# One product of a projection and one transpose in another order, and other matmuls ahead of the first slot

## Chip, core and metric

The kernel runs on one core of a Trainium2 chip. The metric is the device time in microseconds (us), the median of several runs. In the profile PE is TensorE's matmuls, PEld its weight loads, DVE is VectorE, ACT is ScalarE, POOL is GpSimd and SP is SyncE, which here only issues transfers. L474 is line 474 of the kernel before the change.

## The reference

One transformer block on 8 sequences of 256 tokens with 512 features, all in float32:

```python
def _L0_attn_ref(hidden_states, w_qkv, w_o):
    ...
    qkv = hidden_states @ w_qkv
    q = qkv[..., :NH * D].reshape(B, S, NKV, G, D)
    k = qkv[..., NH * D:NH * D + NKV * D].reshape(B, S, NKV, D)
    v = qkv[..., NH * D + NKV * D:].reshape(B, S, NKV, D)
    scores = jnp.einsum('bqhgd,bkhd->bhgqk', q, k) * scale
    ...
    bias = -slopes[:, :, None, None] * sqrt_dist
    bias = jnp.where(rel[None, None] >= 0, bias, -jnp.inf)
    attn = jax.nn.softmax(scores + bias[None], axis=-1)
    out = jnp.einsum('bhgqk,bkhd->bqhgd', attn, v).reshape(B, S, NH * D)
    return out @ w_o
...
x = x + _L0_attn_ref(_layernorm(x, axis=-1), L0_attn_w_qkv, L0_attn_w_o)
x = x + _L0_ffn_ref(_layernorm(x, axis=-1), L0_ffn_weight, L0_ffn_bias, L0_ffn_centroids, L0_ffn_assignments)
```

There are 32 query heads in 8 groups of 4, each group with one head of keys and values, and D is 128. The second half is a dense 512 x 512 layer whose rows and columns are masked by a softmax over 64 centroids.

## The kernel before, in words

**Work and slots.** The tokens are handled in 4 pairs of sequences (`p`), and within a pair by group of heads (`kv`). A pair and a group make a `g` (32 of them), and `g` with one of its two sequences (`bb`) makes a unit `u` (64). The main loop runs over `u`; one turn is called a slot, and `slot = u % 16` is its place in its pair. Even slots have `bb == 0`. A slot works on three units at once: the scores of unit `u`, the softmax of unit `u - 1`, and the attention product and output projection of unit `u - 2`.

**Order.** The order of every engine's queue is written by hand (`manual_schedule`): an engine runs its instructions in the order in which the calls stand in the loop's body, and semaphores make it wait for the others. The body is a list of short calls: `e(i)` and `qq(i)` are steps of the projections to keys or values and to queries, `av(i)` (`attend`) the two attention products, `w(i)` steps of the output projection, `f` and `norm` steps of the feed-forward layer and the layer norm, `x(i)` transposes of the next pair's tokens.

**Products.** Each projection is done in Strassen's form (Winograd's variant), with seven block products instead of eight. Its factors are blocks and sums of blocks (`FACTORS`, L130). For the output projection (`project_out`, L461) these are:

- product 1: raw blocks of oT and wo, bank `ps_oa`; ACT copies it to `snap` (L489)
- product 2: raw blocks too, bank `ps_ob`; DVE adds it to x2 (L494)
- product 5: first sum of oT (POOL, L112) by a sum of wo, bank `ps_oc`; DVE adds it (L500)
- products 6, 7 and 4: accumulated into `ps_oa` after each copy of it; product 3: accumulated into `ps_oc`.

oT is written by DVE (L456) out of the attention products, times one over the sums of the softmax. `av(1)` then gives POOL the four sums of oT (L112 to L118). Banks of PSUM for `av`, product 2, product 5 and the like come from one pool of three that rotate; `aw`, `aq` and `tp` have one bank each.

**Joint transpose.** `max_and_old` and `sum_old` leave DVE's maxima of unit `u` and sums of unit `u - 1` in one tile r (L393, L394, L396). `rows()` (`over_quadrants`, L399) has PE transpose both at once (tp_r, L403), DVE reduce them (L407, L410), and SP write them to HBM (row_hbm, L412) and read them back broadcast over all partitions (bc, L421). In the next slot POOL (L428) and DVE (L431) subtract the maxima, ACT takes exp (L759), and L456 uses the sums.

**Tail of a slot.** Before the change, an even slot ends with

```python
            f(2), norm(0), e(5), e(4), qq(6), e(3), x(0), w(1), x(1), sum_old(), w(5, 6), norm(1), qq(7), w(2)
            rows(), behind_rows(), w(7, 3), norm(3), w(4)
```

and an odd one likewise, with `qq(3)` in place of `qq(7)`. `qq(7)` is drained by an ACT copy, `qq(3)` by a DVE add (L170).

**Start.** While the first tokens and weights load, PE multiplies a 128 x 128 tile of ones by itself 14 times (L625) into `tp1`. Then it transposes the first tokens (L296) once `xn` is there, and the first projection to keys needs wk from HBM.

Of the kernel before, what the change touches and what calls it, by code (L numbers as in the profile page):

```python
# [25 lines left out]
P = 128  # L26
# [27 lines left out]
def block_kernel(  # L54
# [12 lines left out]
    nc = tc.nc  # L67
# [177 lines left out]
    ones = const.tile([P, P], F32, name="ones")  # L245
# [10 lines left out]
    def norm_stats(*tiles):  # L256

        n = len(tiles)
        mv = small.tile([P, 2, 2], F32, tag="mv", name="mv", bufs=2)[:, :n]
        for j, t in enumerate(tiles):  # L260
            stats = small.tile([P, 6], F32, tag="stats", name=f"stats_{t}")
            nc.vector.bn_stats(stats, x2[t])
            nc.vector.bn_aggr(mv[:, j], stats)
        return mv, tiles

    def norm_root(found):

        mv, tiles = found
        rstd = small.tile([P, 2], F32, tag="rstd", name="rstd", bufs=2)[:, : len(tiles)]
        nc.scalar.activation(rstd, mv[:, :, 1], AF.Sqrt, bias=eps)  # L270
        return mv, tiles, rstd
# [49 lines left out]
    def project_v(p, half, i):  # L321

        if i == 0:
            v_sb[p, half] = work.tile([P, TPP, 512], F32, tag="v", name="v", bufs=2)
        v = v_sb[p, half]
        return strassen("v", "aw", wv[p, half], xB[p],
                        lambda w, x: [(slice(0, HH), x[:, c, ts(i, P)], w[:, c, :]) for c in range(2)],
                        [v[:, n * 2 + i, ts(m, HH)] for m in range(2) for n in range(2)], HH)

    def project_k(p, j):  # L330

        kT = kT_sb[p, j] = work.tile([P, 2, PT_TOK], F32, tag="kT", name="kT", bufs=2)
        return strassen("k", "aw", wk[p, j], xB[p],
                        lambda w, x: [(slice(0, S), w[:, c, :], x[:, c, :]) for c in range(2)],
                        [kT[:, m, ts(n, S)] for m in range(2) for n in range(2)], S)
# [175 lines left out]
    def ffn_transpose(t, tag="xnT", **kw):  # L511
        xnT_sb[t] = work.tile([P, NC_H, P], F32, tag=tag, name=f"xnT_{tag}")
        transpose_into(xnT_sb[t], xn_sb[t], t, **kw)
# [19 lines left out]
    def ffn_second(t, w_ffn):  # L533

        second = p_sc.tile([P, 512], F32, tag="sc", name="ps_lg")
        ffn_product(t, w_ffn, HH, HH + NCL, second)
        ffn_sb[t] = second[:, HH : HH + NCL]
        y_sb[t] = [None, second[:, :HH]]

    def ffn_first(t, w_ffn):  # L540
        first = p_acc.tile([P, 512], F32, tag="acc", name="ps_f")
        ffn_product(t, w_ffn, 0, HH, first)
        y_sb[t][0] = first[:, :HH]
# [77 lines left out]
    nc.scalar.activation(warm, eps, AF.Sqrt)  # L621
    tp1 = p_sc.tile([P, 512], F32, tag="sc", name="tpx_1")
    tp2 = p_sc.tile([P, 512], F32, tag="sc", name="tpx_2")
    for i in range(14):
        nc.tensor.matmul(tp1[:, :P], lhsT=ones, rhs=ones, start=True, stop=True)  # L625
    found0 = norm_root(norm_stats(0))
    found1 = norm_root(norm_stats(1))
    norm_write(norm_scale(found0))
# [33 lines left out]
    for u in range(NU + 2):  # L662
        g, bb = divmod(u, 2)
        p, kv = divmod(g, NKV)
        slot = u % SPP
# [19 lines left out]
        e, qq = nothing, nothing  # L685
        if own and u > 0 and slot in (0, 1, 8, 9):
            e = project_v(p, slot // 8, bb)
        elif own and slot in (3, 7, 11):
            e = project_k(p, (slot + 1) // 4)
        elif more_p and slot == 15:  # L690
            e = project_k(p + 1, 0)
        if more_q:
            if bb == 0:
                q = project_q(g + 1)
            qq = q
        ww = {}

        def w(*steps):
            for i in steps:
                if out_:  # L700
                    if i == 1:
                        ww[0] = project_out(u - 2)
                    ww[0](i)


        t_ffn = None
        if own and 3 <= slot < 7 and 0 < p < NPAIR - 1:
            t_ffn = (p - 1) * TPP + slot - 3
        if u >= NU - 2:
            t_ffn = first_late + u - (NU - 2)  # L710

        def f(part):
            if t_ffn is not None:
                if part == 0:
                    ffn_transpose(t_ffn)
                elif part == 1:
                    ffn_second(t_ffn, w_ffn)
                elif part == 1.5:
                    ffn_first(t_ffn, w_ffn)
                    ffn_max(t_ffn)  # L720
                    ffn_exp(t_ffn)
                elif part == 2:
                    ffn_bias_add(t_ffn, y_late[:, t_ffn % TPP, :] if t_ffn >= first_late else None)
                else:
                    ffn_hits(t_ffn)
                    ffn_qsel(t_ffn)
                    ffn_end(t_ffn)
# [12 lines left out]
        def norm(part):  # L740
            nonlocal found
            if t_norm is not None:
                found = (lambda _: norm_stats(t_norm, t_norm + 1), norm_root, norm_scale, norm_write)[part](found)
# [17 lines left out]
        def sum_old():  # L761
            if old:
                over_keys(s_sb[u - 1], r, 1, ALU.add)
# [3 lines left out]
        def rows_max():  # L767
            if alone:
                over_quadrants(u, r, True, False)

        def rows():
            if old:
                over_quadrants(u, r, own and not alone, True)

        def behind_rows():

            f(3)
            norm(2)
            if own and (slot == 7 or slot == 15 and more_p):
                sum_weights(ve, wv, (p, 1) if slot == 7 else (p + 1, 0), HH, "S1 S2")  # L780
            if more_p and slot == 13:
                sum_x(p + 1, "T1 T2")
# [7 lines left out]
        def x(i):  # L790
            if more_p and slot in (11, 12):
                norm_tile(p + 1, 2 * (slot - 11) + i)

        if u == 0:
            k(3), max_and_old()
            sum_weights(ve, wv, (0, 0), HH, "")
            e = project_v(0, 0, 0)
            q_first("5p"), e(1), q_first(5), e(2), rows_max(), q_first(3)
            a_sums(ve, wv[0, 0])
            qq(1), e(6), qq(2), e(7), e(5), qq(6), e(4), e(3), qq(7)  # L800
        elif u == 1:
            e(1), qq(4), e(2), max_and_old(), sum_old(), e(6), qq(5), e(7), e(5), e(4), e(3), qq(3), rows()
        elif bb == 0 and own:
            qq(1), e(1), max_and_old(), e(2), f(0), av(0), e(6), exp_old(), av(1), more_sums(), f(1), rows_max(), f(1.5), e(7), qq(2)
            if u == 4:
                onehot_of_columns(asg)
            f(2), norm(0), e(5), e(4), qq(6), e(3), x(0), w(1), x(1), sum_old(), w(5, 6), norm(1), qq(7), w(2)
            rows(), behind_rows(), w(7, 3), norm(3), w(4)
        elif u < NU - 1:
            e(1), qq(4), e(2), max_and_old(), f(0), e(6), av(0), exp_old(), e(7), av(1), f(1), f(1.5), e(5), qq(5)  # L810
            f(2), norm(0), e(4), e(3), x(0), w(1), x(1), sum_old(), w(5, 6), norm(1), qq(3), w(2)
            rows(), behind_rows()
            if u == NU - 3:
                found_late = norm_scale(norm_root(found_late))
            w(7, 3), norm(3), w(4)
        elif own:

            max_and_old(), f(0), av(0), exp_old(), av(1), rows_max(), f(1), f(1.5)
            f(2), w(1), sum_old(), w(5, 6), w(2)
            rows(), subtract_max(u, 0), subtract_max(u, 1)  # L820
            w(7)
            norm_write(found_late)
            nc.scalar.activation(s_sb[u], s_sb[u], AF.Exp)
            w(3), w(4)
            t_old = t_ffn
        elif bb == 0:
            sum_old(), av(0), f(0), av(1), f(1), rows()
            ffn_first(t_ffn, w_ffn), w(1, 5)
            ffn_max(t_ffn), ffn_exp(t_ffn)
            f(2), w(6)  # L830
            flush_adds()
            ffn_hits(t_old), ffn_qsel(t_old), ffn_end(t_old)
            w(2, 7)
            flush_adds()
            w(3, 4)
            found = norm_stats(last, last + 1)
            t_old = t_ffn
        else:
            av(0), f(0), ffn_hits(t_old), ffn_qsel(t_old)
            found = norm_scale(norm_root(found))  # L840
            av(1), norm_write(found, tags=("y", "y")), f(1), ffn_end(t_old)
            ffn_max(t_ffn), ffn_exp(t_ffn)
            w(1, 2, 5, 6, 3)
            found = norm_root(norm_stats(last + 2))
            w(7)
            ffn_transpose(last, "bc")
            ffn_transpose(last + 1, "snap", tp=p_long.tile([P, 512], F32, tag="aq", name="tpx_late"))
            norm_write(norm_scale(found))
            ffn_hits(t_ffn), w(4), ffn_qsel(t_ffn)
            normalise(norm_stats(last + 3))  # L850
            ffn_first(t_ffn, w_ffn)
# [145 lines left out]
```

## Time and profile before

| what | value |
|---|---|
| median of 3 runs (lowest to highest) | 1418.16 us (1415.27 to 1418.52) |
| the profiled execution, and its span | 1418.65 us, 1416.8 us |
| TensorE clock granted | 0.999 of full |
| product 1 (L474, ps_oa from oT; with product 7), records | 512, 133.0 us |
| product 2 (L474, ps_ob), records | 256, 65.7 us |
| product 5 (L474, ps_oc from wo_t), records | 256, 66.9 us |
| L428 (POOL), 64 times | 152.2 us, 2378 ns each, idle before it 143.0 us |
| ones (L625), records | 28, 5.1 us |

Every float32 matmul leaves two records, each with its own weight load. A line of the timeline gives the start, the time from the first start to the last end, the engine, line, operation and tiles, the count, and in brackets the idle time of the engine before it and what ended it. A line of the list of waits gives the total, how often and the longest. A line of the windows gives the length, PE's and PEld's busy time with their counts of records, the granted clock, the share of the DMA engines and GB/s.

### The profile page before, as it was taken

How to read it: one execution, taken by the hardware profiler on the slowest of the kernel's cores; microseconds unless marked ns; L12 is line 12 of the kernel's file. 1: busy time of each engine (PE TensorE's matmuls, PEld its weight loads, DVE VectorE, ACT ScalarE, POOL GpSimd, SP SyncE). 2: the span in 40 equal slices, each digit the busy share in tenths (PEclk: the TensorE clock that was granted, in tenths of full speed). 3: DMA queues.
4: the chain of work that ended last, by engine and by line, in shares of the span. 5: the costliest groups of instructions: out<-in, count | busy, mean ns of one | idle time of the engine just before them, and what ended most of it. 6: DMA issues, size and time to landing. Idle time of an engine off the chain costs nothing.

```text
span 1416.8 us, 16579 instructions
## 1 busy us (share of the span) xinstructions
PE 1398.6 (99%) x5867; PEld 1083.9 (77%) x5867; DVE 925.0 (65%) x1724; ACT 370.4 (26%) x649; POOL 872.8 (62%) x878
## 2 busy tenths in 40 slices
PE   9999999999999999999999999999999999999997
PEld 7777878767878777777787777877787777777775
DVE  5557656686566665668655666566766566566877
ACT  3222223411232222242213222233121212222332
POOL 6477758767465654668656465565755767476562
PEclk9999999999999999999999999999999999999999
DMA  5335343343242534424334345343314243324344
GB/s 198 125 105 176 112 136 132 134 149 133 92 168 75 179 140 159 146 88 140 133 100 157 113 140 179 120 164 144 136 64 149 99 170 119 135 76 166 120 145 153
DMA packets 87312, 190.20 MB, mean 134 GB/s; under 512 B 11616, under 2 KB 20064, under 8 KB 87232
## 3 DMA queue, kind: packets, MB, share of 16 engines
q1 hardware_dynamic: 86464, 187.85, 38.8%
q10 hardware_dynamic: 720, 1.18, 0.2%
q8 instruction: 47, 0.77, 0.2%
q14 instruction: 33, 0.27, 0.1%
q0 software_dynamic: 48, 0.13, 0.0%
HBM read 176.03 MB, written 13.11 MB: 133 GB/s over the span
## 4 chain that ended last, share of the span: by engine, by line
PE 90%; DVE 5%; issue 1%; DMA 1%; POOL 1%; ACT 0%; SPq 0%; POOLq 0%; DVEq 0%
PE ps_oa L474 14%; PE ps_qa L145 14%; PE ps_oc L474 8%; PE sc L376 7%; PE ps_qc L145 7%; PE av L452 7%; PE ps_ka L145 4%; PE ps_ob L474 4%; PE sc L382 4%; PE ps_va L145 4%; PE av L453 3%; PE ps_qb L145 3%; PE ps_kc L145 2%; PE ps_vc L145 2%; PE ps_lg L520 2%; PE ps_f L520 2%
## 5 line engine op out<-in xcount | busy, mean ns | idle before, releaser
L428 POOL TENSOR_TENSOR s<-s,bc 128x1024 f32<-128x1024 f32 x64 | 152.2, 2378 | 143.0 <-DMA bc<-row_hbm 142.8
L506 POOL TENSOR_TENSOR x<-x,snap 128x256 f32<-128x256 f32 x189 | 135.7, 733 | 162.9 <-DVE x L494 93.1
L393 DVE TRANSPOSE_TENSOR_REDUCE r<-s 128x32 f32<-128x1024 f32 x128 | 157.9, 1234 | 5.5 <-ACT s L759 4.5
L112 POOL TENSOR_TENSOR o_s<-oT 128x256 f32<-128x256 f32 x64 | 48.0, 750 | 184.1 <-DVE oT L456 184.1
L161 ACT COPY qT<-ps_qa 128x512 f32<-128x512 f32 x128 | 74.6, 583 | 285.3 <-PE ps_qa L145 285.3
L489 ACT COPY snap<-ps_oa 128x256 f32<-128x256 f32 x189 | 70.3, 372 | 273.0 <-PE ps_oa L474 272.9
L474 PE MATMUL ps_oa<-wo,oT 128*128 128x256 f32 x512 | 133.0, 382 | 2.3 <-DVE oT L456 2.3
L759 ACT ACTIVATE s<-s 128x1536 f32<-128x1536 f32 x62 | 92.0, 1484 | 149.1 <-DVE s L431 137.1
L452 PE MATMUL av<-s,v 128*128 128x512 f32 x256 | 130.8, 593 | 0.0
L145 PE MATMUL ps_qa<-xT,wq 128*128 128x256 f32 x512 | 121.1, 380 | 0.0
L376 PE MATMUL sc<-qT,kT 128*128 128x512 f32 x256 | 120.4, 593 | 0.0
L145 PEld LDWEIGHTS ps_qa<-xT,wq 128*128 128x128 f32 x512 | 97.4, 190 | 25.9 <-issue 14.3
L378 DVE SCALAR_TENSOR_TENSOR s<-sc,alibi 128x512 f32<-128x512 f32 x128 | 88.0, 691 | 32.0 <-PE sc L376 31.2
L474 PEld LDWEIGHTS ps_oa<-wo,oT 128*128 128x128 f32 x512 | 90.9, 191 | 21.1 <-DVE oT L456 5.4
L384 DVE SCALAR_TENSOR_TENSOR s<-sc,alibi 128x512 f32<-128x512 f32 x64 | 44.3, 691 | 81.7 <-PE sc L382 81.7
L453 PEld LDWEIGHTS av<-s,v 128*128 128x128 f32 x256 | 48.7, 190 | 61.1 <-issue 61.1
L456 DVE TENSOR_TENSOR oT<-av,bc 128x512 f32<-128x512 f32 x128 | 84.0, 682 | 14.9 <-PE av L453 10.4
L394 DVE TRANSPOSE_TENSOR_REDUCE r<-s 128x16 f32<-128x512 f32 x128 | 85.6, 668 | 0.0
L453 PE MATMUL av<-s,v 128*128 128x256 f32 x256 | 76.2, 380 | 0.0
L376 PEld LDWEIGHTS sc<-qT,kT 128*128 128x128 f32 x256 | 48.6, 190 | 34.0 <-issue 29.1
L494 DVE TENSOR_TENSOR x<-x,ps_ob 128x256 f32<-128x256 f32 x64 | 27.0, 421 | 71.7 <-PE ps_ob L474 71.7
L474 PE MATMUL ps_oc<-wo_t,o_s 128*128 128x256 f32 x256 | 66.9, 384 | 2.6 <-POOL o_s L112 2.5
(195 smaller groups left out, 2962.4 us busy)
## 6 DMA issues: line engine op xcount, KB each, us to landing
bc<-row_hbm SPq DMA_DIRECT2D x128, 512.0 KB, 4.9
wq<-in_w_qkv SPq DMA_DIRECT2D x32, 1024.0 KB, 7.7
wo<-in_w_o SPq DMA_DIRECT2D x32, 1024.0 KB, 7.9
alibi<-al_hbm SPq DMA_DIRECT2D x24, 512.0 KB, 8.3
wk<-in_w_qkv SPq DMA_DIRECT2D x16, 512.0 KB, 9.3
wv<-in_w_qkv SPq DMA_DIRECT2D x8, 1024.0 KB, 10.8
x<-in_x SPq DMA_DIRECT2D x16, 256.0 KB, 9.1
al_hbm<-alibi SPq DMA_DIRECT2D x8, 512.0 KB, 9.0
```

The lines of the kernel that those rows point to most:

```text
L145: nc.tensor.matmul(bank[:, cols], lhsT=lhsT, rhs=rhs, start=first and j == 0, stop=j == len(mms) - 1, skip_group_check=True)
L376: nc.tensor.matmul(sc, lhsT=kT[:, t0 : t0 + P], rhs=qT[:, hh : hh + 2, t0 : t0 + S], start=True, stop=True)
L378: nc.vector.scalar_tensor_tensor(s[:, hh * S : (hh + 2) * S], sc, D ** -0.5, bias[:, hh : hh + 2, :].rearrange("p h q -> p (h q)"), ALU.mu ...
L393: nc.vector.tensor_reduce(first, s[:, :K0].rearrange("p (j q) -> p j q", q=32), AX.X, op, apply_transpose=True)
L394: nc.vector.tensor_reduce(second, s[:, K0:].rearrange("p (j q) -> p j q", q=32), AX.X, op, apply_transpose=True)
L428: gp(k0, k0, mx, sub)
L452: nc.tensor.matmul(av, lhsT=v[:, i0, vc], rhs=pT[:, hh * S : (hh + 2) * S], start=True, stop=False)
L453: nc.tensor.matmul(av3[:, :, P:S], lhsT=v[:, i0 + 1, vc], rhs=pT[:, K0 + hh * P : K0 + (hh + 2) * P].rearrange("p (h q) -> p h q", h=2), s ...
L456: ve(oT[:, e].rearrange("p k m q -> p k (m q)"), av3, inv[:, hh : hh + 2, :], ALU.mult)
L474: nc.tensor.matmul(bank[:, :HH], lhsT=x[:, e, :], rhs=y[:, e, :], start=first and e == 0, stop=e == 1, skip_group_check=True)
L506: gp(c, c, s, ALU.add)
L759: nc.scalar.activation(s_sb[u - 1], s_sb[u - 1], AF.Exp)
```

## The change

In every slot but the first two and the last three, the output projection's product 2 is called directly behind product 1, ahead of products 5 and 6. In even slots 4 and 12 of a pair, where no feed-forward tile is in work and `u > 4` (units 12, 28, 44, 52 and 60), `rows()` is called ahead of `qq(7)`, not behind it. At the start, 14 matmuls of ones become 18: 6 as before, 6 over half of the rows of the array (64 of contraction), in turn upper and lower half and into two banks, and 6 over half of its columns (64 outputs), in turn into the lower and upper partitions of one bank.

```diff
-    for i in range(14):
+    for i in range(6):
         nc.tensor.matmul(tp1[:, :P], lhsT=ones, rhs=ones, start=True, stop=True)
+    for i in range(6):
+        h = slice(i % 2 * 64, i % 2 * 64 + 64)
+        nc.tensor.matmul((tp1, tp2)[i % 2][:, :P], lhsT=ones[h, :], rhs=ones[h, :], start=True, stop=True)
+    for i in range(6):
+        h = slice(i % 2 * 64, i % 2 * 64 + 64)
+        nc.tensor.matmul(tp1[h, :P], lhsT=ones[:, :64], rhs=ones, start=True, stop=True)
...
-            f(2), norm(0), e(5), e(4), qq(6), e(3), x(0), w(1), x(1), sum_old(), w(5, 6), norm(1), qq(7), w(2)
-            rows(), behind_rows(), w(7, 3), norm(3), w(4)
+            f(2), norm(0), e(5), e(4), qq(6), e(3), x(0), w(1), x(1), sum_old(), w(2, 5, 6), norm(1)
+
+            if slot in (4, 12) and t_ffn is None and u > 4:
+                rows(), qq(7)
+            else:
+                qq(7), rows()
+            behind_rows(), w(7, 3), norm(3), w(4)
...
-            f(2), norm(0), e(4), e(3), x(0), w(1), x(1), sum_old(), w(5, 6), norm(1), qq(3), w(2)
+            f(2), norm(0), e(4), e(3), x(0), w(1), x(1), sum_old(), w(2, 5, 6), norm(1), qq(3)
             rows(), behind_rows()
```

## The prediction

> **What bounds the kernel.** I read the busy times first, then the chain of waits, then who waited for whom on PE, and last the timeline around the longest of those waits.
>
> ```profile
> PE 1398.6 (99%) x5867; PEld 1083.9 (77%) x5867; DVE 925.0 (65%) x1724; ACT 370.4 (26%) x649; POOL 872.8 (62%) x878
> PE 90%; DVE 5%; issue 1%; DMA 1%; POOL 1%; ACT 0%; SPq 0%; POOLq 0%; DVEq 0%
> ...
> PE ps_oc L474 <- POOL o_s L112: 2.5, 9, 0.5
> PE ps_oa L474 <- DVE oT L456: 2.3, 2, 1.4
> PE ps_ka L145 <- DMA wk<-in_w_qkv: 1.4, 1, 1.4
> ...
> PE ps_oa L474 <- ACT snap L489: 0.5, 1, 0.5
> ```
>
> PE is busy almost all the time and its work is the same before and after, save for the ones at the start. So the change can only win what PE loses in waits, and lose where it makes new ones. The list says where PE waits: product 5 of the projection (ps_oc, from o_s) for POOL's first sum, and product 1 (ps_oa, from oT) for DVE. But these numbers are too small, since a matmul's end is modelled and the first one after a wait also comes late. I therefore measure from start to start. An undisturbed product of two 256-column matmuls (four records) starts 0.86 us after the one before (302.83 to 303.69 in the timeline). Whatever two starts lie further apart is lost. Here is the worst place, units 13 and 14 (a unit is one slot of the loop, about 21 us):
>
> ```profile
> 292.33 2.35 POOL L428 TENSOR_TENSOR s<-s,bc 128x1024 f32<-128x1024 f32 x1 [5.26 <-DMA bc<-row_hbm]
> 292.73 1.98 DVE L396 TENSOR_TENSOR r<-r 128x16 f32<-128x16 f32 x1
> 294.63 0.68 DVE L431 TENSOR_TENSOR s<-s,bc 128x512 f32<-128x512 f32 x1
> 295.23 1.27 DVE L456 TENSOR_TENSOR oT<-av,bc 128x512 f32<-128x512 f32 x2
> ...
> 295.97 1.30 PE L474 MATMUL ps_oa<-wo,oT 128*128 128x256 f32 x4 [1.44 <-DVE oT L456]
> ...
> 297.43 1.13 PE L474 MATMUL ps_oc<-wo_t,o_s 128*128 128x256 f32 x4 [0.17 <-POOL o_s L112]
> ...
> 301.85 0.27 PE L403 MATMUL tp_r<-ident,r 128*64 128x128 f32 x1
> ...
> 302.05 0.42 DVE L494 TENSOR_TENSOR x<-x,ps_ob 128x256 f32<-128x256 f32 x1 [0.18 <-PE ps_ob L474]
> 302.39 0.57 DVE L407 TENSOR_REDUCE row<-tp_r 32x32 f32<-32x128 f32 x2
> ...
> 315.24 1.06 PE L474 MATMUL ps_oa<-wo,oT 128*128 128x256 f32 x4
> ...
> 316.77 1.13 PE L474 MATMUL ps_oc<-wo_t,o_s 128*128 128x256 f32 x4 [0.48 <-POOL o_s L112]
> ```
>
> The reader should see a chain. The broadcast rows land; POOL subtracts (L428); DVE's L396, a median 0.25 us, takes 1.98 us and ends with L428; L431 and the two L456 follow; only then can product 1 start, and product 5 must also wait for POOL's sum of oT. In unit 14 product 1 is in time, but product 5 starts 1.53 us after it instead of 0.86, product 6 1.14 us later and the next step 0.97 us: 0.67 + 0.28 + 0.11 = 1.06 us lost.
>
> **Part 1, product 2 behind product 1.** It removes and adds no instruction. Product 2 (ps_ob) reads oT and raw wo, as product 1 does, so it is ready when product 1 is. It puts 0.86 us of PE work between product 1 and product 5. Surplus of the starts from product 1 to the step behind product 6, slot by slot: unit 2 1.03 (of it 0.70 before product 6, where the ACT copy of the bank is late), unit 5 0.44, unit 13 0.44, unit 14 1.02, unit 29 0.44, unit 30 1.02, unit 45 0.44, unit 46 1.02, unit 50 0.37, units 53 and 61 0.44 each: 7.1 us. The latest sum ends 1.48 us after product 1's start (unit 14), and product 5 will start 1.72 us after it. So all 7.1 us go, and what is late next is the joint transpose (below).
> What the filler covered before: in odd slots the third product of the queries now ends just ahead of the transpose instead of product 2; the PE time from sum_old to the transpose is unchanged. DVE's queue changes: product 2's add (L494, 0.42 us) moves ahead of product 5's add and is done early. In even slots L407 then follows the transpose at once, about 0.25 us sooner. In odd slots L407 stands behind the queries' add L170 (0.69 us), so the rows leave 0.69 - 0.42 = 0.27 us later. The SP transfers row_hbm and bc follow with them; nothing else on SP, POOL or ACT changes its order. PSUM's rotating banks: product 2 now takes the bank that product 5 took, and product 5 the next one. In slots without another projection that bank was av's, which DVE emptied before product 1 could start; in slots with one it was read by an add some 1.7 us earlier. I take nothing; up to one restart (0.10 us) in each of 60 slots, 6 us, is the outer end, and there is nothing to gain.
>
> **Part 2, the joint transpose ahead of the queries' product 7** applies to units 12, 28, 44, 52 and 60. Product 7 is eight records, 1.73 us, so the rows come 1.73 + 0.25 = about 2.0 us sooner. Their r is ready 3.2 to 3.7 us before the transpose now (end of L396 against the start of tp_r), so it does not wait. Product 7's ACT copy comes 0.1 us later and is needed 20 us on.
> In unit 13 L428 waited 5.26 us for bc; it will end near 292.7, L396 will run in 0.25 us behind L394, and oT's first half is there at about 294.2, when PE is free (294.37). Lost there before: 1.60 + 0.10 + 0.06 + 0.10 = 1.87 us. In unit 53 the same: 0.99 + 0.10 + 0.06 + 0.10 = 1.26 us. In units 29, 45 and 61 DVE's line from L384 to L456 is dense already and bc not what it waits for: nothing. Together 3.1 us.
>
> **What is given back.** Slots 14, 30 and 46 have a joint transpose whose r is ready only 0.98 us before it, at the end of a DVE line that starts from L428, and L428 there stands behind a POOL queue without a gap since the sums of the slot before. PE can run ahead by no more than that: in units 29+30 and 45+46 0.95 us each instead of 1.46, in 13+14 about 2.7 instead of 3.33 (POOL starts 1.75 us sooner there). That is 1.0 + 0.6. Near the end the chain goes from unit 61's transpose through row_hbm (3.22 us), bc (4.15) and L428 (2.87) to unit 62's; unit 61 is odd, so 0.27 us more. Given back: 1.9 us.
>
> **Part 3, the ones.** 14 matmuls become 18: four more of full length by the nearest row.
>
> ```profile
> 4.00:4.50 0.50, 0.50 (x4) 0.50 (x4) 1.00 1.03 365
> ...
> 5.00:5.50 0.50, 0.50 (x7) 0.50 (x7) 1.00 1.01 279
> ```
>
> These windows of L625 show the rate: four records in half a microsecond (0.213 us each) until about 4.6 us, then 0.110 us each, though the clock column shows 1.00 from the start. By this row the six full ones take until 3.73, four tiled records until 4.6, the other 20 another 2.2 us: end near 6.8 to 7.0 instead of 6.1. A half-used array is no shorter by the nearest row (a 64-wide tp_r occupies PE 0.109 us, like a full 128-column transpose). The Trainium skill, TensorEngine Tiling (Array Packing), Key Properties, says otherwise on both sides: tiles run in parallel, but changing the mode drains the engine. In parallel the ones would end at about 5.6 us plus two drains. Either way PE then waits: the first transposes need xn (6.35), and the first product needs wk, which lands at 8.84. The row makes the transposes 0.5 us late, and the copies that follow end at about 8.75 instead of 8.2. Cost 0 by both; without wk's cover it would be 0.5 us.
> The rule that speaks against it is TensorE: Matmul & The Clock Gate, Part 1: the fast clock is released after a window of some 3.4 us in which PE was busy (here some 3.6 us after the first matmul). If half-used tiles do not count as busy, the release slips by one window to about 8.0: the tiled records take 5.1 us, the transposes double, and the first product starts near 11.3 instead of 8.97, an estimate of +2.3 us from that page's window. I take 0, since the six full ones and the tiled ones keep PE without a gap as before; the ends are 0 and +2.3.
>
> **Sum.** -7.1 - 3.1 + 1.9 + 0 = -8.3 us. The profiled execution took 1418.65 us (span 1416.8), 0.5 above the median of 1418.16; from its own time, 1410.3.
>
> **Rivals.** (a) *Given back at once*, in slots that I did not name: POOL and DVE are 62 and 65% busy, and units 5, 6, 14, 50 and 54 have product 1 only 0.2 to 0.8 us behind oT, so PE that comes sooner may just wait in the next slot. For: POOL's gapless queue into slots 6 and 14. Against: most slots have 2 to 5 us there. If half of the 8.3 goes, 1414.5. (b) *Clock released late*: 1410.3 + 2.3 = 1412.6. (c) *The other side: a bank wait in every slot.* Product 5 now takes a bank one step earlier in the rotation. If its release came late each time, it would cost one record and one restart, 0.22 + 0.10 = 0.32 us, in 60 slots: +19, so 1429. It decides from 8.3/60 = 0.14 us per slot. For: the banks rotate by three and one of them is held from product 5 to product 3. Against: DVE waits for PE, not the reverse, at the adds that empty them (v L170 behind ps_vc 32.2 us in 16 waits). (d) *It doesn't do what it says*: the rows are moved, but another part of the chain (POOL's L428, row_hbm's round trip) ends last. Then part 2's 3.1 us stay: 1413.4. The changed program's order does have product 2 behind product 1 in every slot.
>
> **Numbers.** A change under about 0.3%, 4.3 us, can't be told from none here; faster means under 1413.9. Forecast 0.62, (a) 0.14, (b) 0.08, (c) 0.07, (d) 0.09. Nearly all of the forecast, (b) and (d) is faster, and some 0.05 of (a): 0.80 in all; (c) is slower; the rest is the same, 0.13. The range from 1406.8 (nothing given back, and 1.5 us for the spread of runs) to 1414.8 takes in all but (c) and the outer half of (a).
>
> **What would show it.** Right: no PE wait for POOL o_s and none for ACT snap at L474; units 13 and 53 without a wait for oT; L428 of unit 13 ending before L396 is due; a short wait of about 0.3 us at tp_r in units 14, 30 and 46; the first product still at about 9.0 us. Wrong: waits of PE for a DVE add at ps_oc, a first product at 11 us, or waits for oT in units 6, 14 or 54 as long as those removed.

## The result and the profile after

The changed kernel took **1410.31 us**, the median of 6 runs (1409.77 to 1412.19), beside 1418.58 us for the kernel before (6 runs, 1415.27 to 1421.03). The ratio is 0.9943, with an interval of 0.9928 to 0.9958: 8.1 us faster. The profiled execution took 1410.37 us, with a span of 1408.5.

The busy times and the shares of the chain, from the page of the changed kernel:

```profile
PE 1394.1 (99%) x5875; PEld 1085.8 (77%) x5875; DVE 923.3 (66%) x1724; ACT 370.3 (26%) x649; POOL 874.0 (62%) x878
...
PE 94%; DVE 3%; POOL 1%; DMA 1%; issue 1%; ACT 0%; SPq 0%; DVEq 0%; ACTq 0%; POOLq 0%
```

PE has eight records more (the ones), and its share of the chain went from 90 to 94%, DVE's from 5 to 3%: what DVE had on the path is partly gone. Who waited for whom on PE (total, times, longest):

```profile
PE ps_ka L145 <- DMA wk<-in_w_qkv: 1.4, 1, 1.4
PE ps_va L145 <- DVE wv L116: 1.3, 2, 0.8
...
PE tp_r L403 <- DVE r L396: 0.6, 2, 0.4
...
PE tpx L296 <- ACT xT L297: 0.3, 1, 0.3
```

The waits for POOL's o_s, for ACT's snap and for oT are all gone. In their place stands a wait that was not in the list before: the projection to values waits for wv, a sum that DVE makes (L116).

A wait in this list is smaller than what is lost, so I made a ledger for each trace: for every record of PE, the time to the next start, less the usual spacing of that record (0.216 us for 256 columns, 0.429 for 512). Only surpluses over 15 ns count; each goes to what PE starts next.

| surplus of PE's starts, us | before | after | before, 2nd trace | after, 2nd trace |
|---|---|---|---|---|
| output projection behind product 1 | 8.36 | 0.92 | 8.95 | 1.10 |
| product 1, waiting for oT | 2.64 | 0.13 | 2.17 | 0.32 |
| banks of the scores (sc) | 1.51 | 0.46 | 1.51 | 0.47 |
| joint transpose (tp_r) | 0.50 | 0.94 | 0.37 | 2.34 |
| projection to values, waiting for wv | 0 | 1.61 | 0.26 | 0.93 |
| transposes of tokens (tpx) | 0.57 | 0.83 | 0.34 | 1.06 |
| first 20 us, tail, the rest | 9.81 | 9.99 | 10.71 | 10.14 |
| sum | 23.37 | 14.88 | 24.31 | 16.35 |
| span | 1416.8 | 1408.5 | 1417.8 | 1410.0 |

The ledger falls by 8.5 us and the span by 8.3, so it accounts for the result. Here is the place that the prediction began with, units 13 and 14, in the timeline of the changed kernel:

```profile
289.22 2.36 POOL L428 TENSOR_TENSOR s<-s,bc 128x1024 f32<-128x1024 f32 x1 [2.82 <-DMA bc<-row_hbm]
...
292.06 0.17 DVE L396 TENSOR_TENSOR r<-r 128x16 f32<-128x16 f32 x1
292.15 0.68 DVE L431 TENSOR_TENSOR s<-s,bc 128x512 f32<-128x512 f32 x1
292.75 1.28 DVE L456 TENSOR_TENSOR oT<-av,bc 128x512 f32<-128x512 f32 x2
...
293.69 1.09 PE L474 MATMUL ps_oa<-wo,oT 128*128 128x256 f32 x4
...
294.62 1.03 PE L474 MATMUL ps_ob<-wo,oT 128*128 128x256 f32 x4
...
295.48 1.03 PE L474 MATMUL ps_oc<-wo_t,o_s 128*128 128x256 f32 x4
...
308.61 0.28 DVE L396 TENSOR_TENSOR r<-r 128x16 f32<-128x16 f32 x1
308.81 0.68 DVE L431 TENSOR_TENSOR s<-s,bc 128x512 f32<-128x512 f32 x1
308.81 2.89 POOL L428 TENSOR_TENSOR s<-s,bc 128x1024 f32<-128x1024 f32 x1
...
311.97 1.03 PE L474 MATMUL ps_oa<-wo,oT 128*128 128x256 f32 x4
```

In unit 13 POOL's L428 starts at 289.22 instead of 292.33 and is over (291.58) before DVE wants L396, which takes 0.17 us instead of 1.98. Product 1 has its oT, product 2 follows, and product 5 starts 0.86 us behind product 2, without a wait. In unit 14 something else has changed: DVE's L396 now comes 0.20 us *ahead* of L428. In the kernel before, L396 started 0.53 us behind L428 and took 1.86 us:

```profile
311.35 2.36 POOL L428 TENSOR_TENSOR s<-s,bc 128x1024 f32<-128x1024 f32 x1
...
311.88 1.86 DVE L396 TENSOR_TENSOR r<-r 128x16 f32<-128x16 f32 x1
```

The new wait is in units 16 and 56. The timeline before unit 16's fourth product of the projection to values:

```profile
341.47 0.45 SPq L412 DMA_DIRECT2D row_hbm<-row  x1
...
345.00 0.80 SPq L421 DMA_DIRECT2D bc<-row_hbm  x2
...
349.05 2.35 POOL L428 TENSOR_TENSOR s<-s,bc 128x1024 f32<-128x1024 f32 x1 [1.59 <-DMA bc<-row_hbm]
...
350.22 1.22 DVE L396 TENSOR_TENSOR r<-r 128x16 f32<-128x16 f32 x1
...
351.36 0.68 DVE L431 TENSOR_TENSOR s<-s,bc 128x512 f32<-128x512 f32 x1
...
351.96 0.68 DVE L116 TENSOR_TENSOR wv<-wv 128x512 f32<-128x512 f32 x1
...
352.79 1.10 PE L145 MATMUL ps_va<-wv,xT 128*128 128x256 f32 x4 [0.77 <-DVE wv L116]
```

SP issues the write of the row at 341.47 and the read back only at 345.00, when the write has landed: 3.5 us. In the kernel before, the same pair is 1.7 us apart:

```profile
345.52 0.45 SPq L412 DMA_DIRECT2D row_hbm<-row  x1
...
347.24 0.80 SPq L421 DMA_DIRECT2D bc<-row_hbm  x2
```

Everything behind it is late by the difference: L428, then L396, which again ends with L428, then the sum for wv. So two questions were open. Which part of the change is worth what? And why do some rows take twice as long?

### The profile page after: what moved, and what is told of

The parts are those of the page before. It is cut to its first block, busy times and chain, and to the rows that moved or that the text cites. A ratio compares the mean times of both kernels' runs of the same rounds, so it can differ in the third digit from the quotient of the medians.

```text
span 1408.5 us, 16598 instructions
## 1 busy us (share of the span) xinstructions
PE 1394.1 (99%) x5875; PEld 1085.8 (77%) x5875; DVE 923.3 (66%) x1724; ACT 370.3 (26%) x649; POOL 874.0 (62%) x878
## 4 chain that ended last, share of the span: by engine, by line
PE 94%; DVE 3%; POOL 1%; DMA 1%; issue 1%; ACT 0%; SPq 0%; DVEq 0%; ACTq 0%; POOLq 0%
PE ps_oa L474 15%; PE ps_qa L145 15%; PE ps_qc L145 8%; PE sc L376 8%; PE ps_oc L474 8%; PE av L452 7%; PE sc L382 4%; PE ps_ka L145 4%; PE ps_ob L474 4%; PE av L453 4%; PE ps_va L145 4%; PE ps_qb L145 4%; PE ps_vc L145 2%; PE ps_kc L145 2%; PE ps_lg L520 2%; PE ps_f L520 2%
## 5 line engine op out<-in xcount | busy, mean ns | idle before, releaser
L428 POOL TENSOR_TENSOR s<-s,bc 128x1024 f32<-128x1024 f32 x64 | 152.9, 2388 | 119.5 <-DMA bc<-row_hbm 119.4
L500 DVE TENSOR_TENSOR x<-x,ps_oc 128x256 f32<-128x256 f32 x128 | 53.2, 416 | 37.1 <-PE ps_oc L474 36.3
L396 DVE TENSOR_TENSOR r<-r 128x16 f32<-128x16 f32 x128 | 66.8, 522 | 4.4
```

What stands on the lines that cost most here:

```text
L428: gp(k0, k0, mx, sub)
```

## The experiments

Each run is given as a ratio to the kernel before on the same chip, with its interval.

**The parts, alone and together.** My theory was the prediction's sum; the rival, that the parts share a gain or that one of them does nothing. Part 1 alone:

```diff
-... sum_old(), w(5, 6), norm(1), qq(7), w(2)
+... sum_old(), w(2, 5, 6), norm(1), qq(7)
-... sum_old(), w(5, 6), norm(1), qq(3), w(2)
+... sum_old(), w(2, 5, 6), norm(1), qq(3)
```

> Product 2 behind product 1 alone. Forecast's theory (waits for o_s go in every execution): 7.1 us less than before, of which up to 1.6 us is given back at the joint transposes of units 14, 30, 46 and 0.3 at the end: ratio 0.9955 to 0.9965, no wait of PE for o_s left, the waits for oT of units 13 and 53 still there. Rival theory (late trips of the row through HBM fall elsewhere in each execution): the same 6 to 7 us, but the waits for oT need not be in units 13 and 53 again.

Measured: 1411.64 us, **0.9941 [0.9929, 0.9954]**, 8.4 us by the ratio. That is more than the 0.9955 to 0.9965 expected. The waits for o_s and snap are gone, and with them most of the waits for oT (0.34 us in the ledger, from 2.64), which were expected to stay in units 13 and 53; that they need not was the rival.

Part 2 alone:

```diff
-... w(5, 6), norm(1), qq(7), w(2)
-rows(), behind_rows(), ...
+... w(5, 6), norm(1)
+if slot in (4, 12) and t_ffn is None and u > 4:
+    w(2), rows(), qq(7)
+else:
+    qq(7), w(2), rows()
+behind_rows(), ...
```

> Joint transpose ahead of the queries' product 7 in units 12, 28, 44, 52, 60 alone. Forecast's theory: the waits for oT in units 13 and 53 go, 3.1 us, ratio 0.998. Rival theory: those two waits were late row trips of one execution (7.2 to 7.8 us from row_hbm's issue to L428 instead of 5.7), which another execution need not have at these places: the median moves by under 1.5 us, ratio 0.999 to 1.0, and single waits for oT or wv stand at other units.

Measured: 1415.98 us, 0.9972 [0.9961, 0.9983], 4.0 us. The waits for oT are gone (0.16 us in the ledger), those for o_s stay, as the list of waits of this kernel shows:

```profile
PE ps_oc L474 <- POOL o_s L112: 2.5, 9, 0.5
```

Part 3 alone, the loops of ones as in the change:

```diff
-    for i in range(14):
+    for i in range(6):
...
```

> The other ones alone. Forecast: the first product still starts when wk lands, 8.8 to 9.0 us, and the time is that of before within 0.5 us, ratio 1.000. Rival: the clock is released earlier or later than before and the time moves by up to 2.3 us; or the shorter warm-up (it ended at 6.1 to 6.3 us in the changed kernel) wins the 0.45 us that PE waited ahead of the first transpose.

Measured: 1419.76 us, 0.9998 [0.9990, 1.0007]: nothing. Its list of waits has two lines that matter below:

```profile
PE ps_oa L474 <- DVE oT L456: 1.6, 1, 1.6
...
PE ps_va L145 <- DVE wv L116: 0.8, 2, 0.4
```

The order is that of before, yet PE waits for oT in one unit instead of two, and for wv in units 16 and 56.

Parts 1 and 2 together, with the 14 full ones of before:

```diff
-    for i in range(6):
+    for i in range(14):
...
```

> The change without the new ones. Forecast: as the whole change, ratio 0.994 to 0.9945. Rival (the ones do more than the trace of their stretch shows): at least 1.5 us slower than the whole change, ratio 0.9955 or more.

Measured: 1409.78 us, 0.9932 [0.9919, 0.9944], 9.7 us. The parts add up to 12.4, so they seem to share 2.7 us. That is the size of the waits for oT, 2.64 us in the trace of before, which are gone with either part; but each of the three figures is known to some 1.7 us only. On top of part 1, part 2 brings about 1 us, and the intervals of the two ratios overlap. So do those of this run and of the whole change (0.9943): whether the ones cost up to 1.5 us there is not settled by the times.

**Is it any filler, or this product?** If part 1 works only by giving POOL time, any product of PE between product 1 and product 5 will do. So the last query product goes there instead:

```diff
-... sum_old(), w(5, 6), norm(1), qq(7), w(2)
+... sum_old(), qq(7), w(5, 6), norm(1), w(2)
```

with `qq(3)` likewise in odd slots.

> Order before, with the queries' product 7 or 3 (1.73 us of PE) moved ahead of product 5 instead of product 2; product 2 stays last ahead of the transpose. Theory (any PE work between product 1 and product 5 hides POOL's sums): waits for o_s gone except in unit 62, where there is no queries' product, and 6 to 8 us less than before, ratio 0.994 to 0.9955, like prod2_only. Rival (product 2's place itself matters, by its DVE add or its bank): at least 2 us slower than prod2_only.

Measured: 1420.97 us, 1.0007 [0.9999, 1.0015]: no gain, though PE waits for o_s no longer. The list of waits of this kernel says why:

```profile
PE ps_qa L145 <- ACT qT L161: 2.1, 5, 1.3
```

In even slots the query product accumulates into a bank that ACT still has to copy, in odd ones, by the program, into one that DVE still has to add. In the ledger the surplus behind product 1 stands at 7.27 us, beside 8.36 before: most of the wait has moved from product 5 to the filler. So the expected theory is wrong for this product. Product 2 reads only what product 1 reads, and starts a bank of its own. What its place or its DVE add do beside that was not tested apart.

**Why are some rows late?** The trip of the row (8 KB, from its issue to its landing) takes 1.7 us in the median (at most 2.2) in most units and 2.5 to 3.8 in some. The DMA view of the kernel before, for a window around unit 12's row (the columns of a queue are packets, MB and its share; of an issue, the size and the time to landing):

```profile
q8 instruction: 1, 0.02, 0.6%
...
row_hbm<-row SPq DMA_DIRECT2D x1, 8.0 KB, 3.4
```

The same view of the same kernel around unit 28's row, which is in time:

```profile
q1 hardware_dynamic: 391, 1.11, 31.9%
issues: line engine op xcount, KB each, median us to landing
...
row_hbm<-row SPq DMA_DIRECT2D x1, 8.0 KB, 1.6
```

In the first window one packet of 16 KB of an instruction queue, q8, is on its way; in the second none. I took all 13 traces of this study together: of 871 writes of rows, 135 had a q8 packet starting within 1.85 us of their issue (a bound read off these data), and 92 of those were late, that is over 2.4 us. Of the other 736 none was. So such a packet goes with every late row, though not every meeting makes a row late.

The queue's kind says that these packets are the program's own instructions. The Trainium skill (Runtime: NRT & Kernel Launch, Instruction fetch mechanics) says that an engine's instructions are fetched by a DMA queue of its sequencer in blocks of 16 KB, 256 instructions, and that the cost of crossing into a new block is mostly hidden. The blocks agree: there are 47 q8 packets, one per 123.5 matmul records of PE (247 with their weight loads). That q8 is PE's queue is my inference from this count; no other engine has so many instructions (DVE, the next, has 1724). The page speaks of the engine that fetches; for the row that meets the fetch it is not hidden. If it is so, PE instructions added at the start move the packets against the slots, and other rows are late. That was tested with more ones, without any tiling, on parts 1 and 2, and with second traces of the kernels before and after:

```diff
-    for i in range(14):
+    for i in range(20):
```

> prod2_rows with 20 full ones instead of 14: 24 more PE instructions ahead of the first slot, hidden behind wk's load (ones end near 7.4 us). Theory (instruction fetch): every later fetch falls about 24 instructions, some 2.6 us of PE work, earlier in the work, so the set of units with a late row is another than 19, 23, 49, 55, and the time moves by what the newly hit units cost, up to 1.5 us either way. Rival: the same units, the time within 0.5 us of prod2_rows.

> The kernel before, unchanged: a second trace. In the first, the write of the rows to HBM (row_hbm) took 3.0 to 3.7 us instead of 1.65 in units 12, 14, 19, 45, 49, 52, 54, 58 and 61, each time with a 16 KB packet of the instruction queue q8 starting 1.0 to 1.6 us after its issue. Theory (the program's own fetch of instructions, set by PE's place in the program, holds the row up): most of these units are late again, and none is late without such a packet. Rival (chance): late units anywhere, also without a packet. Time as before, ratio 1.000.

> The changed kernel once more, unaltered: a second trace of it. Theory (which rows' writes are late is set by how many instructions TensorE is given ahead of them, since the packets of the instruction queue come at fixed places of the program): the late writes of the rows fall in about the same units as in the first trace (5, 9, 12, 15, 52, 55, 59), the waits for wv in units 16 and 56 are there again (0.9 and 0.7 us), the one for oT in unit 13 stays under 0.3, the span is within 1 us of 1408.5. Rival (which writes are late is chance of one execution): another set, as between the two traces of the kernel before, and the waits of units 16 and 56 gone or elsewhere.

| kernel | ones | units whose row is late |
|---|---|---|
| parts 1 and 2 | 14 | 19, 23, 49, 55 |
| part 1 alone | 14 | 19, 23, 49, 55 |
| parts 1 and 2 | 20 | 5, 9, 12, 15, 43, 52, 55, 59 |
| part 3 alone | 18 | 2, 5, 9, 12, 14, 15, 18, 38, 55, 58, 59 |
| the change | 18 | 5, 9, 12, 15, 52, 55, 59 |
| the change, second trace | 18 | 5, 9, 12, 15, 52, 55, 59 |
| before | 14 | 12, 14, 19, 45, 49, 52, 54, 58, 61 |
| before, second trace | 14 | 19, 23, 38, 42, 45, 49, 52, 54 |
| part 2 alone | 14 | 14, 18, 19, 23, 38, 42, 45, 49, 58 |
| query product as filler | 14 | 12, 14, 15, 18, 58, 59 |

The kernel with 20 full ones has the change's list and one unit more, and the two traces of the change agree; so there the number of PE's instructions decides, not the tiling. The order of the work counts too: with 14 ones, other orders have other lists. In the kernel before, the list varies between executions: five of the nine units of the first trace are late again, and three others are. What else decides there is open. Times: 1412.62 us (0.9948 [0.9935, 0.9960]) with 20 ones, by the ratios some 2 us above that of 14, where 1.5 was expected at most, though the intervals overlap; part of it is the start, whose first product begins at 9.3 us instead of 8.95 with 14 (it lies between 8.1 and 9.3 in the 13 traces); 1419.41 (0.9996 [0.9987, 1.0004]) for before again; 1411.94 (0.9941 [0.9927, 0.9955]) for the change again. There the waits for wv came back in the same units, but smaller than expected, 0.63 and 0.30 us before the first record instead of 0.93 and 0.68.

The second trace of the change is 1.5 us longer, where 1 us was expected at most. One wait near the end is as long as that. The timeline of the first trace there:

```profile
1349.58 0.17 DVE L396 TENSOR_TENSOR r<-r 128x16 f32<-128x16 f32 x1
...
1349.65 2.36 POOL L428 TENSOR_TENSOR s<-s,bc 128x1024 f32<-128x1024 f32 x1 [2.13 <-DMA bc<-row_hbm]
...
1350.30 0.27 PE L403 MATMUL tp_r<-ident,r 128*64 128x128 f32 x1
```

And that of the second:

```profile
1349.14 2.34 POOL L428 TENSOR_TENSOR s<-s,bc 128x1024 f32<-128x1024 f32 x1 [1.99 <-DMA bc<-row_hbm]
1349.22 2.30 DVE L396 TENSOR_TENSOR r<-r 128x16 f32<-128x16 f32 x1
...
1351.66 0.27 PE L403 MATMUL tp_r<-ident,r 128*64 128x128 f32 x1 [1.56 <-DVE r L396]
```

In the first, L396 starts 0.07 us ahead of L428 and takes 0.17 us. In the second bc landed earlier, L428 starts 0.08 us ahead of L396, and L396 ends with it: 2.30 us, and PE waits 1.56. A transfer that came *sooner* made the kernel slower. The Trainium skill (SBUF — State Buffer, Who interferes with whom) has the rule: a DVE instruction with two SBUF inputs and a GpSimd instruction that reads SBUF block each other, and the order of issue decides who waits. The traces agree: in all 13, each of the 631 L396 (of 1664) that took over 0.6 us began while a POOL instruction was running, and ended within 0.1 us of the end of one. So does the other side; L428 takes 2.89 us instead of 2.36 in unit 14, where DVE's L431 began with it.

**Can the wait for wv be avoided?** The sum for wv depends on nothing that is made in its slot. So it goes ahead of the scores, with parts 1 and 2 alone, and in the changed kernel itself:

```diff
 def max_and_old():
+    if u > 0 and slot in (0, 8):
+        a_sums(ve, wv[p, slot // 8], "S3 S4")
     scores(u, 2)
...
-    if u > 0 and slot in (0, 8):
-        a_sums(ve, wv[p, slot // 8], "S3 S4")
```

> prod2_rows with DVE's third and fourth sum of wv (slots 0 and 8) ahead of the third scores instead of behind L431. PE's program is that of prod2_rows, so the late rows should again be near units 19, 23, 49 and 55. Theory: PE's waits for wv in slots 24 and 56 (0.8 and 0.4 us with the restarts, units whose rows were late) go, 1.2 us in the trace, ratio to before about 0.9925. Rival: DVE's 1.4 us moved ahead make another wait (oT or tp_r in slots 0 and 8) and nothing is won.

> The changed kernel with VectorE's fourth sum for wv in slots 0 and 8 ahead of the scores' product of that slot, instead of behind it. Theory: the 1.6 us that TensorE waits for wv in units 16 and 56 is all that the change gives back there, so the span goes from 1408.5 to about 1406.9, and the late writes stay where they are, since TensorE's instructions are the same. Rival: the late rows of units 15 and 55 hold VectorE up anyway, and the wait moves to the next product that needs VectorE (the scores' bank or the joint transpose): within 0.5 us of 1408.5.

Measured: 1408.18 us (1407.89 to 1409.12), **0.9917 [0.9904, 0.9931]**, span 1406.0, without the ones of the change; 1409.20, 0.9920 [0.9906, 0.9933], with them, beside 0.9941 for the change on the same chip. In both the wait for wv is 0 and the late rows stay where they were. The profiled span of the second, 1409.9, missed the 1406.9 expected: it was the slowest of five, with the 1.7 us wait near the end as above and 1.0 us more in the first 20 us. The median fell by 2.7 us against the change, of which 0.9 to 1.6 are the waits seen. That the waits go is shown by the traces; what they are worth is not settled by the times, since both intervals overlap with those of the kernels without the early sum (0.9932 and 0.9941). The first of these two has the lowest median of the study.

Then the joint transpose ahead of the query product in all even slots:

```diff
-if slot in (4, 12) and t_ffn is None and u > 4:
+if u > 4:
     rows(), qq(7)
```

> The change without its new ones, with the early sum for wv, and the joint transpose ahead of the last query product in every even slot from unit 6 on, not in two kinds of slots alone. Theory: nothing is left to win, since the waits for oT are 0.1 us in all in that kernel, and every joint transpose that is moved loses a query product of cover behind VectorE's sum over the keys: TensorE waits for r at the transpose in more units, 0.3 to 0.5 us in each of some 20 units at the worst: span 1406 to 1414, most likely 1408 (two more than 1406.0). Rival: VectorE's sum is done well ahead in these slots too, and the earlier rows also shorten the waits for wv, the scores' bank and the token transposes: span 1405 to 1406.

Measured: 1412.97 us, 0.9949 [0.9936, 0.9961], span 1410.3: by the ratios 4.5 us slower than with two kinds of slots. The list of its waits:

```profile
PE tp_r L403 <- DVE r L396: 4.0, 5, 1.1
```

Three of these, 1.25 us each in the ledger, are in units 14, 30 and 46, where the query product was the cover behind which DVE finished r. So the expected theory held, in three units rather than twenty; moving the transpose pays only where r is ready well ahead.

## Why the prediction came out right

The time of 1410.3 was met to the tenth, but the terms were not; the agreement is partly luck, since two executions of the changed kernel differ by more, and since a gain of 1.0 us that it did not name made up for what part 2 and the give-back came short.

- **Part 1, -7.1.** Right in mechanism and size: the ledger has -7.4 for that group, and no wait for o_s or snap is left. Alone it brings 8.4 us, since the waits for oT went as well.
- **Part 2, -3.1.** Right in what it does: units 13 and 53 have no wait for oT, although unit 12's row is late in the changed kernel too (2.8 us). The size holds for part 2 alone (4.0 [2.4, 5.5]). What failed is adding it to part 1: the 1.87 and 1.26 us of units 13 and 53 were read as a property of the order, and were in part the lateness of the rows of units 12 and 52. Product 1 of unit 13 starts 1.60 and 1.72 us late in the two traces with the order of before in which unit 12's row is late, (before, and part 3 alone) and 0.53 in the one in which it is not (before, second trace); unit 53's 0.99 and 1.60 with unit 52's row late, not at all without. In the traces of part 1 alone and of part 2 alone neither row is late, so what each saves at oT there is in part this chance; that part 2 protects units 13 and 53 from a late row is seen only in the changed kernel. Part 1 with the 18 ones and without part 2, which would show the wait, was not run.
- **Given back, +1.9.** The amount was about right, the place wrong. No wait came at the transposes of units 14, 30 and 46. The step assumed that L428 would go on holding DVE up there; instead L396 got in 0.20 us ahead of it, and the waits for the scores' banks of those slots went as well (-1.0 us, not forecast). What was given back came for wv in units 16 and 56 (+1.6), at the transposes (+0.4 and +0.3), and 0.2 elsewhere: 2.5 us, or 1.5 net of the banks. This is rival (a) in place and far under its price. Not all of it is PE's lead: with part 3 alone, in the order of before, units 16 and 56 wait 1.1 us for wv too, and the rows of units 15 and 55 are late there as well.
- **Part 3, 0.** Right: the first product starts at 8.84 us. But my row was the wrong one. The PE timeline of the changed kernel (L628 has the ones over half of the rows, L631 those over half of the columns):

```profile
3.87 1.65 PE L628 MATMUL tpx<-ones 64*128 64x128 f32 x12
5.45 0.92 PE L631 MATMUL tpx<-ones 128*64 128x128 f32 x12
6.31 1.09 PE L296 MATMUL tpx<-ident,xn 128*128 128x128 f32 x8
```

  Twelve records over half of the rows took 1.58 us from first start to next form, 0.13 each against 0.21 to 0.24 for a full one just before; twelve over half of the columns 0.86, 0.07 each against 0.11. Two neighbouring records, one in each half, start 6 to 7 ns apart, and such a pair takes what one full record takes (0.21 us at the slow clock, 0.11 at the full one); each change of form took 0.10 to 0.14 us more. Both fit what the prediction's page of the Trainium skill, TensorEngine Tiling (Array Packing), Key Properties, says: tiles run in parallel, and a change of mode drains the engine. The ones ended at 6.3 us instead of 6.8 to 7.0. Rival (b) did not come: the clock was full from 5.6 us, ahead of the transposes. The side effect that I had no term for is that eight more records move the fetches, and so which rows are late.
- **Rival (c)**, a bank wait in every slot, did not occur: behind product 1, 0.92 us are left in all slots together. (The slots with the new order are 61, units 2 to 62, not 60, which changes no term.)

## What to carry to other kernels

A filler that is to hide a wait must be ready itself, its output bank included. Here the product that reads the same inputs as the one ahead of it was, and another one was not. Two parts that each remove the same wait do not add: before summing, ask which wait each of them ends, and whether that wait is there in a second trace. Where two engines block each other, a lead of 0.1 us decided over 1 to 2 us. So ask which of the two starts first before making one of them faster; moving the short instruction well ahead should help, but was not tried here.

## What was not expected of the hardware

- A write of 8 KB that meets a 16 KB packet of the program's own fetch landed in 2.5 to 3.8 us instead of 1.7 in 92 of 135 such meetings in 13 traces, and in none of the 736 writes without one. Eight matmul records more at the start moved the affected units.
- In the second trace of the kernel before, PE's clock halved for 3.4 us behind the 1.4 us wait for oT in unit 53. The windows of PE there (length, busy time and records, granted clock, share of the DMA engines, GB/s):

```profile
1156.00:1158.00 2.00, 1.49 (x5) 1.00 1.03 386
1158.00:1160.00 2.00, 2.00 (x7) 0.60 1.07 377
1160.00:1162.00 2.00, 2.00 (x7) 0.55 0.65 241
1162.00:1164.00 2.00, 2.00 (x11) 1.00 0.00 0
```

  From 1158.40 to 1161.81 the records stand 0.427 us apart instead of 0.216: seven of them, and one at either end in part, some 1.7 us more than the wait itself cost. The same wait of 1.4 us in unit 13 of the first trace cost no clock. The Trainium skill (TensorE: Matmul & The Clock Gate, Part 1) speaks of a free-running window of some 3.4 us, and of an idle window as what brings the slow clock; the length of the drop agrees, but here a pause of 1.4 us, less than half a window, with gaps of 0.06 to 0.34 us behind it, was enough. When it is enough was not tried.
- The moment of the full clock at the start did not follow the ones. The first matmul starts at 1.0 us in all 13 traces; the clock was full from 3.9 to 6.1 us in the nine with full ones, and from 3.9 to 6.2 in the four with half tiles, so it varies between executions.
